# A four-layer graph network on one core: edge units in two fp16 parts, tanh moved in front of the scatter, a softmax without row maxima

## The chip, the core and the metric

The kernel runs on one core of a Trainium2 chip. The engines named below are TensorE (PE for its matmuls, PEld for its weight loads), VectorE (DVE), ScalarE (ACT), GpSimd (POOL) and SyncE (SP, which issues the DMAs here). Each engine works through its own queue in order, and the engines wait for each other with semaphores. The metric is the device time in microseconds of one execution; the value for a kernel is the median of its runs.

## What is computed

The input is x, 16 batches of 1024 nodes with 128 features, and adj, 16 weighted adjacency matrices of 1024 x 1024, of which some 1.5% are not zero. Four graph layers follow each other, each fed with the positive part of a layer norm of x and added to x. The change touches the third and the fourth:

```python
# layer 2, for l in range(2):
a = einsum('bnd,de->bne', x, We1[l, :D])
b = einsum('bnd,de->bne', x, We1[l, D:])
h = relu(a[:, :, None, :] + b[:, None, :, :] + be1[l])
scores = sigmoid(squeeze(h @ We2[l], -1) + be2[l])
messages = einsum('bnm,bmd->bnd', adjacency * scores, x)
...
# layer 3
e = (Wh1 + swapaxes(Wh2, 1, 2)) * (A + eye(N))
e = where(e >= 0, e, 0.2 * e)
scores = where(A + eye(N) > 0, e, -1e12)
h_prime = matmul(softmax(scores, axis=2), Wh)
```

The scores of layer 2 matter only where adj is not zero, so the kernel computes them for the edges alone.

## The kernel before

The adjacency matrix of a batch is cut into 128 x 128 tiles. A tile and its mirror image share their pattern, so there are 28 pairs off the diagonal and 8 diagonal tiles, 36 "buckets" in 9 groups of four (`GROUPS`: two diagonal groups, seven others). Each bucket has a fixed number of slots for its edges, 320 off the diagonal and 480 on it. For each batch `first` computes layers 0 and 1, counts the edges, and builds for each bucket one-hot matrices in fp8: `on`, `om` (node by slot) and their transposes `onT`, `omT`.

For each layer l of layer 2, `round` runs over the nine groups. `split` computes the two node terms a and b with We1 in float32 and cuts them into two fp16 parts (a rounded one and the rest, L715 and L716). `Group.gather` adds, for one bucket and one direction (two directions off the diagonal), the terms of the two ends of each edge with four fp16-by-fp8 matmuls into a PSUM bank `pre` (L810, L814; two banks in turn), and ScalarE takes the relu with the bias be1 into a float32 tile `hid` (L826). Each batch and layer has 64 such tiles. `Group.dots` takes four of them at a time, one set, and multiplies each with We2: the stationary operand is a 128 x 32 window of `slide`, in which only one column is not zero, so each product lands on one row of a strip of 32 rows of the bank `sc` (L838). The four strips are four column groups of the array. `Group.ends` copies the finished scores with be2 into `srow` (L856). In the next group's time `scores` turns them by matmul (L867), cuts each into two fp16 halves that lie in one 32-bit word, `u` (L872, L873), and spreads them over the one-hot matrix, `val` (L890, on VectorE): a multiplication of 0 or 1 by the word. `scatter` puts the scores in their places of a dense 128 x 512 tile with fp16 matmuls (L914), ScalarE takes tanh of it (L922), VectorE adds 1 and multiplies with the adjacency (L923), and `messages` multiplies with x in float32 (L930). A factor of 0.5 on the way out (L953) makes tanh a sigmoid.

`update` is the rest of a layer of layer 2. `last` does the second update and layer 3 (`layer3`), whose attention goes by 8 strips of 128 x 1024: L360 to L367 on VectorE, Exp on ScalarE with a sum along the row (L368), eight transposes (L372), eight matmuls (L243).

`run` weaves three lanes of program text for each batch b: `main(b)`, `last(b - 1)` and `first(b + 1)`. Each yields the cost of the piece it has just written, and `weave` takes the lane that has used the smallest share of its total (MAIN_US, LAST_US, FIRST_US). From this text each engine's order is laid out ahead of the run; the trace shows pieces of one lane, such as a set of dots, cut by pieces of another. Each lane has its own PSUM bank or banks ("pre" with two for m, "a" and "c" with one each).

At the end a flag says whether a bucket had more edges than slots; if so, a second path (`Pairs`) computes everything densely.

Of the kernel before, what the change touches and what calls it, by code (L numbers as in the profile page):

```python
# [22 lines left out]
C_OFF = 320  # L23
C_DIAG = 480

S_SCALE = 256.0
S_MAX = 60000.0

# [11 lines left out]

MAIN_US = 248.0
FIRST_US = 112.0
# [7 lines left out]
def tile_four_gnn_layers(  # L50
# [81 lines left out]
    nc.vector.tensor_copy(a2_bc, a3_sb[:, 1:2].to_broadcast([P, P]))  # L132

    slide = const.tile([P, L, 2 * G - 1], F32, name="slide")
    nc.vector.memset(slide, 0.0)
    for l in range(L):
        nc.vector.tensor_copy(slide[:, l, G - 1 : G], we2_sb[:, l : l + 1])

# [30 lines left out]
    class Layers:  # L169
# [121 lines left out]
        def update(self, l, xf, xfT, msgT, dst, name):  # L291
# [40 lines left out]
            yield 3  # L332

        def layer3(self, xt, row, name):

# [19 lines left out]
            for t in range(T):  # L355
                at = row(t)
                own = at[:, t * P : (t + 1) * P]
                nc.vector.tensor_add(own, own, ident)
                e = flat(self.scratch(f"e_{name}_{t}"))
                nc.vector.scalar_tensor_tensor(  # L360
                    e, wh2, wh1[:, t : t + 1], at, op0=OP.add, op1=OP.mult
                )
                nc.vector.tensor_scalar(at, at, 0.0, L3_NEG, op0=OP.is_le, op1=OP.mult)
                nc.vector.scalar_tensor_tensor(e, e, L3_ALPHA, e, op0=OP.mult, op1=OP.max)
                nc.vector.tensor_add(e, e, at)
                nmax = self.small([P, 1], "nmax", f"nmax_{name}_{t}")
                nc.vector.tensor_reduce(nmax, e, axis=AX.X, op=OP.max, negate=True)  # L367
                nc.scalar.activation(e, e, AF.Exp, bias=nmax, accum_out=rsum[:, 0, t : t + 1])  # L368
                attT = self.scratch(f"attT_{name}_{t}")
                for ks, ps in self.halves(f"attT_ps_{name}_{t}"):  # L370
                    for i, k in enumerate(ks):
                        nc.tensor.transpose(ps[:, i], e[:, k * P : (k + 1) * P], ident)  # L372
                    nc.scalar.activation(attT[:, ks[0] : ks[-1] + 1], ps, AF.Copy)
                hp = self.neighbours(attT, wh, f"3_{name}_{t}")
                nc.vector.reciprocal(rsum[:, 1, t : t + 1], rsum[:, 0, t : t + 1])
                nc.vector.tensor_scalar(o[:, t], hp, rsum[:, 1, t : t + 1], None, op0=OP.mult)
                yield 5
            neg = self.scratch(f"neg_{name}")
            nc.vector.tensor_scalar(neg, o, 0.0, None, op0=OP.min)
# [22 lines left out]
    class Batch:  # L402
        pass

    class Edges:
        def __init__(self, stack):
            self.work = stack.enter_context(tc.tile_pool(name="work", bufs=2))
            self.con = stack.enter_context(tc.tile_pool(name="con", bufs=1))
            self.hot = stack.enter_context(tc.tile_pool(name="hot", bufs=1))
            self.dram = stack.enter_context(  # L410
                tc.tile_pool(name="dram", bufs=2, space=bass.MemoryType.DRAM)
            )
            self.psum = stack.enter_context(
                tc.tile_pool(name="psum", bufs=1, space=bass.MemoryType.PSUM)
            )

            own = {"m": ("pre", 2), "a": ("a", 1), "c": ("c", 1)}
            self.m, self.a, self.c = (
                Layers(self.work, v, N_SCRATCH[v], self.psum, [own[v]]) for v in LANES
            )  # L420
            self.alone = [own[v] for v in ("a", "m", "c", "m")]
            self.constants()
# [14 lines left out]
        def constants(self):  # L437
# [32 lines left out]
            self.scale_terms()  # L470
            self.slide = con.tile([P, L, 2 * G - 1], F32, name="slide_s")
            for l in range(L):
                nc.vector.tensor_scalar(
                    self.slide[:, l], slide[:, l], unit[:, 1, l : l + 1], S_SCALE,
                    op0=OP.mult, op1=OP.mult,
                )
            self.be2 = con.tile([P, L], F32, name="be2_s")
            nc.vector.tensor_scalar(self.be2, be2_bc, S_SCALE, None, op0=OP.mult)

# [6 lines left out]
        def scale_terms(self):  # L486
# [18 lines left out]
            for l in range(L):  # L505
# [6 lines left out]
            nc.vector.tensor_reduce(  # L512
                bnd, ps[:, : 2 * L].rearrange("p (l h) -> p l h", h=2), axis=AX.X, op=OP.max
            )
            ps = self.a.one("bound_t")
            nc.tensor.transpose(ps[:L, :P], bnd, ident)
# [19 lines left out]
            nc.vector.tensor_copy(unit.rearrange("p i l -> p (i l)"), ps[:, : 2 * L])  # L536
            scale_layer(0)

        def load(self, lane, src, name):
# [170 lines left out]

        def split(self, xfT, w, name):

            parts = self.work.tile([P, 2, T, 2, D], F16, tag="part", name=f"part_{name}", bufs=1)
            for sl, ps in self.m.both(xfT, w, name):
                nc.scalar.activation(parts[:, 0, sl], ps, AF.Copy)  # L715
# [3 lines left out]
        def round(self, s, l, xf, xfT, name):  # L719


            pa, pb = self.split(xfT, we1_sb[:, l], name)
            msg = self.acc(f"msg_{name}")
# [36 lines left out]
        class Group:  # L760
# [41 lines left out]
            def gather(self, i, pa, pb):  # L802
# [4 lines left out]
                for d, (ra, rb) in enumerate((((pa, t), (pb, u)), ((pb, t), (pa, u)))[: self.nd]):  # L807
# [9 lines left out]
                    if not self.diag:  # L817
                        hid = path.work.tile(
                            [P, C_OFF], F32, tag="hid", name=f"hid_{self.name}_{i}_{d}", bufs=N_HID
                        )  # L820
                    elif i % 2 == 0:
                        self.two = flat(path.m.scratch(f"hid_{self.name}_{i}"))
                        hid = self.two[:, :HALF]
                    else:
                        hid = self.two[:, HALF:]
                    nc.scalar.activation(  # L826
                        hid[:, :c], pre[:, :c], AF.Relu, bias=be1_sb[:, self.l : self.l + 1]
                    )
                    self.hid.append(hid)

            def dots(self):
# [3 lines left out]
                while len(self.hid) - self.done >= J:  # L835
                    r = self.done // J
                    for g in range(J):
                        nc.tensor.matmul(  # L838
                            self.sc[g * G : (g + 1) * G, : self.c],
                            self.path.slide[:, self.l, G - 1 - r : 2 * G - 1 - r],  # L840
                            self.hid[self.done + g][:, : self.c],
                            start=(r == 0), stop=(r == self.per - 1),
                        )
                    self.done += J

            def ends(self):
# [8 lines left out]
                for dst, src in parts:  # L855
                    nc.vector.tensor_scalar(  # L856
                        dst, src, self.path.be2[:, self.l : self.l + 1], S_MAX, op0=OP.add, op1=OP.min
                    )

            def scores(self):  # L860
# [5 lines left out]
                for k in range(ck):  # L866
# [4 lines left out]
                u2 = u.bitcast(F16).rearrange("p (c r h) -> p c r h", r=per, h=2)  # L871
                nc.vector.tensor_scalar(u2[:, :, :, 1], pt, -S_MAX, None, op0=OP.max)  # L872
                nc.vector.scalar_tensor_tensor(  # L873
                    u2[:, :, :, 0], pt, -S_MAX, u2[:, :, :, 1], op0=OP.max, op1=OP.subtract
                )
# [6 lines left out]
                for d in range(self.nd):  # L882
                    for i in range(Q):
                        if i % 2 == 0:
# [4 lines left out]
                        right = (self.s.omT if d else self.s.onT)[self.grp[i]]  # L889
                        nc.vector.tensor_tensor(  # L890
                            pair[:, i % 2, :ck], right[:, :ck],
                            u[:, :, j % J, j // J : j // J + 1].to_broadcast([P, ck, P]), op=OP.mult,
                        )
                        self.val[d, i] = pair[:, i % 2]

            def scatter(self, part):

                each = self.rows // Q  # L900
                for j in range(part * each, (part + 1) * each):
# [16 lines left out]
                    if i == Q - 1:  # L918
                        upd = self.path.work.tile(
                            [P, Q, P], F32, tag="upd", name=f"upd_{self.name}_{d}"  # L920
                        )
                        nc.scalar.activation(upd, self.ps[d], AF.Tanh, scale=0.5 / S_SCALE)  # L922
                        nc.vector.scalar_tensor_tensor(  # L923
                            upd, upd, 1.0, self.adj[:, d * Q : (d + 1) * Q], op0=OP.add, op1=OP.mult
                        )
# [18 lines left out]
        def main(self, s, b):  # L944
# [3 lines left out]
            for l in range(L):  # L948
# [3 lines left out]
                s.msgT = lane.scratch(f"msgT_{name}")  # L952
                nc.vector.tensor_scalar(flat(s.msgT), self.msg, 0.5, None, op0=OP.mult)  # L953
                if l + 1 == L:
# [163 lines left out]
    with ExitStack() as stack:  # L1118
        path = Edges(stack)
        path.run()  # L1120

        over = path.work.tile([P, 2], F32, name="over")
        nc.vector.tensor_scalar(over[:, 0:1], path.most[:, 0:1], 2.0 * C_OFF, None, op0=OP.is_gt)
        nc.vector.tensor_scalar(over[:, 1:2], path.most[:, 1:2], 2.0 * C_DIAG, None, op0=OP.is_gt)
        ps = path.m.one("over_ps")
        nc.tensor.matmul(ps[:1, :2], ident[:, P - 1 : P], over, start=True, stop=True)
        nc.vector.tensor_reduce(flag, ps[:1, :2], axis=AX.X, op=OP.max)

# [41 lines left out]
```

## Time and profile before

| | us |
|---|---|
| median of 3 runs (5927.56 to 5934.77) | 5927.58 |
| profiled execution, its own time | 5932.83 |
| its span, first to last instruction | 5931.1 |
| hid, relu on ScalarE (L826), 2048 times | 1104.1 busy |
| pre, gather on TensorE (L810 and L814), 8192 times | 978.3 and 966.7 busy |
| dots (L838), 512 sets of 8 instructions | 676.1 busy |
| val on VectorE (L890), 2048 times | 606.6 and 440.1 busy |
| tanh behind the scatter on ScalarE (L922), 512 times | 305.7 busy |

The granted clock of TensorE was 0.980 over the span. Busy time counts an instruction from its start to its end; neighbours overlap, and a group's busy time is the time in which at least one of it runs. PE's busy time includes the time in which results leave the array, so it is an upper bound for the work itself. A float32 matmul appears as two instructions. In a line of a group the columns are: engine, operation, output and inputs by the program's names, sizes and types, count, then busy time, mean length in ns, and the engine's idle time just before the group's instructions, with what ended it.

### The profile page before, as it was taken

To read this page: it belongs to the slowest core of one execution; us is meant where nothing else is said; L and a number is where in the kernel's file an instruction comes from. 1 tells how busy PE (TensorE), PEld (TensorE's weight loads), DVE (VectorE), ACT (ScalarE), POOL (GpSimd) and SP (SyncE) were. 2 spreads that over 40 slices of the span, in tenths; PEclk is the share of its full clock that TensorE was granted. 3 is DMA by queue.
4 is the path that set the end of the run, shared out by engine and by line. 5 is a ranking of instruction groups with operands and counts; after the bars stand their busy time and mean duration, and the time that the engine had idled before them with its cause. 6 is when DMAs were issued, how large, how long until landed. Compare 5 with 4: busy or idle time off the path is not lost.

```text
span 5931.1 us, 112266 instructions
## 1 busy us (share of the span) xinstructions
PE 5518.9 (93%) x46080; PEld 3910.8 (66%) x46080; DVE 4248.2 (72%) x8138; ACT 3057.9 (52%) x5859; POOL 173.3 (3%) x105
## 2 busy tenths in 40 slices
PE   4899999999999999999999999999999999999985
PEld 4666667666676666667666676666667666676653
DVE  4566777867678686777867678686777867678665
ACT  2545464554646455474554646455374554646442
POOL 0000000000000000000000000000000000000000
PEclk8999999999999999999999999999999999999997
DMA  5322414233142422414233142432414233142110
GB/s 150 100 83 79 121 58 123 91 100 107 52 138 75 120 91 83 125 58 123 91 97 108 50 139 79 115 96 80 128 58 121 93 97 107 51 139 72 45 63 29
DMA packets 694154, 554.34 MB, mean 93 GB/s; under 512 B 29440, under 2 KB 630144, under 8 KB 693632
## 3 DMA queue, kind: packets, MB, share of 16 engines
q1 hardware_dynamic: 688384, 545.37, 30.8%
q8 instruction: 364, 5.96, 0.4%
q10 hardware_dynamic: 5248, 1.71, 0.2%
q14 instruction: 158, 1.29, 0.1%
HBM read 446.31 MB, written 100.66 MB: 92 GB/s over the span
## 4 chain that ended last, share of the span: by engine, by line
PE 65%; DVE 21%; ACT 5%; DMA 4%; issue 3%; POOL 2%; ACTq 0%; SPq 0%; DVEq 0%; POOLq 0%
PE sc L838 9%; PE p L914 7%; PE pre L810 7%; PE pre L814 7%; PE nb L243 6%; PE msg L930 5%; PE h L301 4%; DVE val L890 3%; PE bb L251 3%; PE pq L692 2%; PE pn L660 2%; PE xn L314 2%; POOL st L207 2%; PE pm L660 2%; PE tn L586 2%
## 5 line engine op out<-in xcount | busy, mean ns | idle before, releaser
L826 ACT ACTIVATE hid<-pre,be_sb 128x320 f32<-128x320 f32 (+1 forms) x2048 | 1104.1, 545 | 925.9 <-PE pre L814 913.1
L810 PE MATMUL pre<-on,part 128*128 128x320 fp8e4 (+1 forms) x4096 | 978.3, 308 | 20.0 <-ACT hid L826 10.5
L814 PE MATMUL pre<-om,part 128*128 128x320 fp8e4 (+1 forms) x4096 | 966.7, 307 | 0.0
L838 PE MATMUL sc<-hid,slide_s 128*32 128x320 f32 (+1 forms) x4096 | 676.1, 461 | 1.6 <-DVE u L873 1.5
L930 PE MATMUL msg<-upd,xf 128*128 128x128 f32 (+3 forms) x2944 | 608.3, 327 | 4.1 <-DVE upd L923 3.8
L890 DVE TENSOR_TENSOR val<-onT,u 128x384 f32<-128x384 fp8e4 (+1 forms) x1152 | 606.6, 580 | 4.3
L810 PEld LDWEIGHTS <-part 128*128 128x128 f16 x4096 | 363.6, 98 | 301.1 <-issue 233.8
L914 PE MATMUL p<-val,omT 128*128 128x128 f16 x6528 | 547.7, 218 | 2.0 <-DVE val L890 0.2
L814 PEld LDWEIGHTS <-part 128*128 128x128 f16 x4096 | 394.9, 98 | 173.5 <-issue 25.0
L914 PEld LDWEIGHTS <-omT 128*128 128x128 fp8e4 x6528 | 441.9, 96 | 68.9 <-issue 19.7
L696 DVE TENSOR_TENSOR omT<-pq,odd_off 128x384 fp8e4<-128x384 f32 x448 | 248.1, 554 | 318.4 <-PE pq L692 312.7
L890 DVE TENSOR_TENSOR val<-omT,u 128x384 f32<-128x384 fp8e4 x896 | 440.1, 549 | 0.0
L923 DVE SCALAR_TENSOR_TENSOR upd<-upd,adj 128x512 f32<-128x512 f32 x512 | 351.5, 686 | 112.3 <-ACT upd L922 108.5
L930 PEld LDWEIGHTS msg<-upd,xf 128*128 128x128 f32 x2944 | 399.4, 191 | 27.0 <-DVE upd L923 8.8
L922 ACT ACTIVATE upd<-p 128x512 f32<-128x512 f32 x512 | 305.7, 597 | 189.8 <-PE p L914 176.9
L856 DVE TENSOR_SCALAR srow<-sc,be_s 128x128 f32<-128x128 f32 (+2 forms) x512 | 217.1, 449 | 242.0 <-PE sc L838 240.0
L703 ACT ACTIVATE om<-pm 128x320 fp8e4<-128x320 f32 (+1 forms) x576 | 266.9, 464 | 212.3 <-PE pm L660 207.5
L689 ACT ACTIVATE onT<-pn 128x384 fp8e4<-128x384 f32 (+1 forms) x576 | 295.1, 513 | 128.0 <-PE pn L660 126.8
L914 PE MATMUL p<-val,onT 128*128 128x128 f16 x4480 | 354.4, 218 | 4.7 <-ACT upd L922 4.6
L914 PEld LDWEIGHTS <-onT 128*128 128x128 fp8e4 x4480 | 294.9, 96 | 49.2 <-issue 20.5
L360 DVE SCALAR_TENSOR_TENSOR e<-wh,wh,a 128x1024 f32<-128x1024 f32 x128 | 163.7, 1279 | 197.9 <-PE attT_ps L372 180.4
L243 PEld LDWEIGHTS nb<-z,ct 128*128 128x128 f32 x2048 | 251.1, 197 | 66.1 <-issue 45.6
(195 smaller groups left out, 9188.4 us busy)
## 6 DMA issues: line engine op xcount, KB each, us to landing
at<-in_adj_dram SPq DMA_DIRECT2D x128, 512.0 KB, 3.9
ct<-in_adj_dram SPq DMA_DIRECT2D x128, 512.0 KB, 4.1
a<-in_adj_dram SPq DMA_DIRECT2D x128, 512.0 KB, 3.4
adjT<-tn SPq DMA_DIRECT2D x128, 512.0 KB, 4.8
l<-adjT SPq DMA_DIRECT2D x128, 512.0 KB, 4.3
adj<-adjT SPq DMA_DIRECT2D x256, 256.0 KB, 3.5
adj<-adjT SPq DMA_DIRECT2D x384, 64.0 KB, 2.9
adj<-adjT SPq DMA_DIRECT2D x128, 192.0 KB, 3.0
```

Of the source, the lines that this page charges most:

```text
L243: nc.tensor.matmul(ps, mat[:, k], z[:, k], start=(k == 0), stop=(k == T - 1))
L689: nc.scalar.activation(onT, pn[:, : ck * P], AF.Copy, saturate=False)
L703: nc.scalar.activation(om, pm[:, :c], AF.Copy, saturate=False)
L810: nc.tensor.matmul(pre[:, :c], ra[0][:, k, ra[1]], on[:, :c], start=(k == 0), stop=False)
L814: nc.tensor.matmul(pre[:, :c], rb[0][:, k, rb[1]], om, start=False, stop=(k == 1))
L826: nc.scalar.activation(hid[:, :c], pre[:, :c], AF.Relu, bias=be1_sb[:, self.l : self.l + 1])
L838: nc.tensor.matmul(self.sc[g * G : (g + 1) * G, : self.c], self.path.slide[:, self.l, G - 1 - r : 2 * G - 1 - r], self.hid[self.done + g][ ...
L890: nc.vector.tensor_tensor(pair[:, i % 2, :ck], right[:, :ck], u[:, :, j % J, j // J : j // J + 1].to_broadcast([P, ck, P]), op=OP.mult,)
L914: nc.tensor.matmul(self.ps[d][:, i], left[:, k], halves[:, k, :, h], start=(k, h) == terms[0], stop=(k, h) == terms[-1],)
L922: nc.scalar.activation(upd, self.ps[d], AF.Tanh, scale=0.5 / S_SCALE)
L923: nc.vector.scalar_tensor_tensor(upd, upd, 1.0, self.adj[:, d * Q : (d + 1) * Q], op0=OP.add, op1=OP.mult)
L930: nc.tensor.matmul(self.msg[:, lo * P : hi * P], self.xf[:, mb], up, start=False, stop=True, skip_group_check=True,)
```

## The change

In words:

- **We2 folded into We1.** Since relu(v) w = sign(w) relu(v |w|), the columns of We1 and be1 are multiplied by |We2| at the start, and `slide` holds only the signs -1, 0 and 1.
- **Edge units in two fp16 parts.** be1 is now added in `split`, on the node term b, by an addition in PSUM. `gather` takes the relu without a bias on ScalarE into an fp16 tile, and the rest (the relu of pre less that part) on VectorE into a second fp16 tile. `dots` multiplies both parts with the signs in fp16.
- **tanh in front of the scatter.** `ends` is a tanh on ScalarE with bias and scale; `scores` cuts tanh times 256 in two halves; behind the scatter ScalarE has nothing to do, and VectorE reads the scatter's bank.
- **val on two engines.** Every second bucket's `val` is made on ScalarE, one activation of 128 columns for each 128 slots.
- **Layer 3 without row maxima** (class `Lane`): no subtraction of the maximum, and the mask is multiplied in behind Exp, with the sum of the row. A further condition of the flag (`fine`) says whether every row sum and its reciprocal are at most 1e30.
- **The weave's weight** MAIN_US is 215 in place of 248. Some constants change with these.

```diff
-MAIN_US = 248.0
+MAIN_US = 215.0
...
+    with tc.tile_pool(name="fold", bufs=1) as fold:
+        mag = fold.tile([P, L, D], F32, name="we2_mag")
+        nc.scalar.dma_start(mag, we2.rearrange("l d o -> (o l) d")[None].broadcast_to([P, L, D]))
+        nc.scalar.activation(mag, mag, AF.Abs)
...
+        for l in range(L):
+            nc.vector.tensor_mul(
+                we1_sb[:, l], we1_sb[:, l], mag[:, l, None, :].to_broadcast([P, 2, D])
+            )
...
+    class Lane(Layers):
...
+        def weights(self, e, at, total, name):
+            nc.vector.scalar_tensor_tensor(e, e, L3_ALPHA, e, op0=OP.mult, op1=OP.max)
+            nc.scalar.activation(e, e, AF.Exp)
+            nc.vector.scalar_tensor_tensor(
+                e, at, 0.0, e, op0=OP.is_gt, op1=OP.mult, accum_out=total
+            )
...
-                nc.vector.tensor_scalar(at, at, 0.0, L3_NEG, op0=OP.is_le, op1=OP.mult)
-                nc.vector.scalar_tensor_tensor(e, e, L3_ALPHA, e, op0=OP.mult, op1=OP.max)
-                nc.vector.tensor_add(e, e, at)
-                nmax = self.small([P, 1], "nmax", f"nmax_{name}_{t}")
-                nc.vector.tensor_reduce(nmax, e, axis=AX.X, op=OP.max, negate=True)
-                nc.scalar.activation(e, e, AF.Exp, bias=nmax, accum_out=rsum[:, 0, t : t + 1])
+                self.weights(e, at, rsum[:, 0, t : t + 1], f"{name}_{t}")
...
-            for sl, ps in self.m.both(xfT, w, name):
+            for sl, ps in self.m.both(xfT, we1_sb[:, l], name):
+                nc.vector.tensor_add(ps[:, :, 1], ps[:, :, 1], over_t(self.be1[:, l], 2))
...
-                            [P, C_OFF], F32, tag="hid", name=f"hid_{self.name}_{i}_{d}", bufs=N_HID
+                            [P, 2, C_OFF], F16, tag="hid", name=f"hid_{self.name}_{i}_{d}", bufs=N_HID
...
-                    nc.scalar.activation(
-                        hid[:, :c], pre[:, :c], AF.Relu, bias=be1_sb[:, self.l : self.l + 1]
+                    nc.scalar.activation(hid[:, 0, :c], pre[:, :c], AF.Relu)
+                    nc.vector.scalar_tensor_tensor(
+                        hid[:, 1, :c], pre[:, :c], 0.0, hid[:, 0, :c], op0=OP.max, op1=OP.subtract
                     )
...
-                    for g in range(J):
-                        nc.tensor.matmul(
-                            self.sc[g * G : (g + 1) * G, : self.c],
-                            self.path.slide[:, self.l, G - 1 - r : 2 * G - 1 - r],
-                            self.hid[self.done + g][:, : self.c],
-                            start=(r == 0), stop=(r == self.per - 1),
-                        )
+                    for v in range(2):
+                        for g in range(J):
+                            nc.tensor.matmul(
+                                self.sc[g * G : (g + 1) * G, : self.c],
+                                self.path.slide[:, self.l, G - 1 - r : 2 * G - 1 - r],
+                                self.hid[self.done + g][:, v, : self.c],
+                                start=(r == 0 and v == 0), stop=(r == self.per - 1 and v == 1),
+                            )
...
-                    nc.vector.tensor_scalar(
-                        dst, src, self.path.be2[:, self.l : self.l + 1], S_MAX, op0=OP.add, op1=OP.min
+                    nc.scalar.activation(
+                        dst, src, AF.Tanh, bias=self.path.be2[:, self.l : self.l + 1],
+                        scale=self.path.down[:, self.l : self.l + 1],
                     )
...
-                        nc.vector.tensor_tensor(
-                            pair[:, i % 2, :ck], right[:, :ck],
-                            u[:, :, j % J, j // J : j // J + 1].to_broadcast([P, ck, P]), op=OP.mult,
-                        )
+                        v = u[:, :, j % J, j // J : j // J + 1]
+                        if i % 2:
+                            for k in range(ck):
+                                nc.scalar.activation(
+                                    pair[:, 1, k], right[:, k], AF.Copy, scale=v[:, k]
+                                )
+                        else:
+                            nc.vector.tensor_tensor(
+                                pair[:, 0, :ck], right[:, :ck], v.to_broadcast([P, ck, P]), op=OP.mult
+                            )
...
-                        nc.scalar.activation(upd, self.ps[d], AF.Tanh, scale=0.5 / S_SCALE)
                         nc.vector.scalar_tensor_tensor(
-                            upd, upd, 1.0, self.adj[:, d * Q : (d + 1) * Q], op0=OP.add, op1=OP.mult
+                            upd, self.ps[d], S_SCALE, self.adj[:, d * Q : (d + 1) * Q],
+                            op0=OP.add, op1=OP.mult,
                         )
```

## The prediction

> **What bounds the kernel now.** I read four views, from coarse to fine. First the page: busy time by engine, and the chain of work that ended last.
>
> ```profile
> PE 5518.9 (93%) x46080; PEld 3910.8 (66%) x46080; DVE 4248.2 (72%) x8138; ACT 3057.9 (52%) x5859; POOL 173.3 (3%) x105
> ...
> PE 65%; DVE 21%; ACT 5%; DMA 4%; issue 3%; POOL 2%; ACTq 0%; SPq 0%; DVEq 0%; POOLq 0%
> ```
>
> TensorE is the bound, VectorE second: of 5931 us the chain runs 65% through PE, 21% (1246 us, 29% of DVE's busy time) through DVE, 5% (297 us, 9.7% of ACT's) through ACT. Second, the same chain in order of time, in the middle of a batch (start, length, work):
>
> ```profile
> 2232.95 0.66 PE sc L838 x2
> 2233.61 0.27 PE pn L660 x3
> 2233.88 0.67 PE sc L838 x6
> ...
> 2237.45 0.50 PE msg L930 x4
> ...
> 2238.25 0.27 PE pre L810 x2
> ...
> 2240.45 0.68 PE sc L838 x8
> ```
>
> Work follows work without gaps. An fp16-by-fp8 pass of 320 columns (pre) takes 0.135. A float32 matmul is two instructions of two passes each: msg's 128-column instruction takes 0.125, where fp16 passes of the scatter take 0.057 (ten in 0.57, elsewhere in this view). Most telling is sc: two, six or eight of its instructions take the same 0.66 to 0.68, so the four strips of 32 columns run side by side, and a burst costs four passes (0.54) plus 0.13. One set (four strips, eight instructions) is often cut in two bursts with other work between. Third, the groups by shape (busy, mean ns, idle before):
>
> ```profile
> L826 ACT ACTIVATE hid<-pre,be_sb 128x320 f32<-128x320 f32 x1792 | 935.7, 529 | 864.6 <-PE pre L814 855.1 <-PE pq L692 2.3 <-PE po L622 0.3
> L838 PE MATMUL sc<-hid,slide_s 128*32 128x320 f32 x3584 | 551.1, 445 | 1.6 <-DVE u L873 1.5
> L890 DVE TENSOR_TENSOR val<-onT,u 128x384 f32<-128x384 fp8e4 x896 | 443.8, 551 | 3.7
> L647 ACT ACTIVATE far<-iota_off,mid 128x384 f16<-128x384 f16 x448 | 267.4, 617 | 4.0 <-DVE on L651 4.0
> L365 DVE TENSOR_TENSOR e<-e,a 128x1024 f32<-128x1024 f32 x128 | 155.5, 1215 | 0.1
> L716 DVE TENSOR_TENSOR part<-bb,part 128x512 f16<-128x512 f32 x128 | 87.1, 687 | 29.2 <-ACT part L715 28.1
> L262 ACT ACTIVATE z<-bb 128x256 f32<-128x256 f32 x64 | 24.5, 383 | 56.5 <-PE bb L251 56.5
> ```
>
> ACT waits for PE before hid: it has room. Fourth, the stretches of one batch (a batch is about 356 us), PE, PEld, DVE, ACT busy of 12:
>
> ```profile
> 2314.00:2326.00 12.00, 11.79 (x83) 6.20 (x80) 5.15 (x10) 5.99 (x12) 0.00 (x0) 1.00 0.01 1
> ...
> 2362.00:2374.00 12.00, 12.00 (x112) 8.78 (x110) 11.46 (x22) 5.69 (x11) 0.00 (x0) 1.00 0.58 168
> ```
>
> In 9 of 30 such stretches DVE is over 11.2 of 12 busy: it has no room there, and much in the others.
>
> **The dots (PE).** 512 sets: 448 of 320 columns (3584/8), 64 of 480. Now busy 551.1 + 125.0 = 676 us; on the chain 8.9% = 528. Afterwards a strip takes two fp16 passes instead of four. In one burst a set costs 2 x 0.135 + 0.13 = 0.40 (480 columns: 0.54), 214 us in all; in two bursts, one per part, 0.53 and 0.67, 280; if each part is cut again, 1.06 and 1.34, 561. Saved: against busy time 462, 396 or 115; against the chain's 528, 314, 248 or a loss of 33. The high part is ready an instruction earlier than the low one, so I expect two bursts, between 396 and 248, nearer the first, since a burst off the chain holds PE too: **-360**.
>
> **The second part (DVE), new:** 2048 scalar_tensor_tensor from PSUM. The nearest row is L716, same types, 687 at 512 columns; L890's forms (551 at 384, 683 at 512) give 1.03 ns a column, so 489 at 320 and 654 at 480: 876 + 167 = 1043. In a run, four val take 1.95, which is 64 ns less each: 912. I take 980.
>
> **What DVE loses:** every second val goes to ACT, half of 1046.7, -523. ends() goes to ACT: -229.7 (107.6 + 76.5 + 45.6). Layer 3 drops L363, L365 and L367 (88.0 + 155.5 + 154.9) and gains one masked multiply with a sum, priced as L364's 1217 ns x 128 = 156, at most 180 with a read of the sum like ACT's 189 ns: -235. split() gains 128 adds of be1, 422 ns each by L263: +54. upd (686 ns) keeps its shape and now reads PSUM; u, msgT likewise: nothing. Sum **+46**, from -22 to +117.
>
> **ACT.** hid loses its bias column; a bias costs 90 ns (L305's 687 against L373's 597 at 512): -184. The odd val become 28 x 3 + 4 x 4 = 100 activations of 128 columns per layer and batch, 3200. No row has this shape. From below L262, PSUM without a column, less 128 columns at 0.86 ns: 276 ns, 883 us. From above L647, SBUF and a column, less 256 at 0.81: 409, 1309 us. It is nearer L647; some overlap between neighbours: 360, 1150 us. tanh in front of the scatter: -305.7 (L922); on the score rows 224 of 256 columns, 224 of 128 and 64 of 480, with two columns each 90: 563, 456, 748 ns, +276. Exp without bias and accumulator: 128 x (90 + 189) = -36. Sum **+900**, from +633 to +1059: ACT to about 3960 us, 70%.
>
> The Trainium skill (ScalarE: Activation LUTs, Rules for kernel authors) advises VectorE, not ScalarE, for a plain multiply, which speaks against this move. In this case's rows it is dear too: about 1.1 us of ACT for 0.55 of DVE. That page's figures (186 ns, 93 a column, 0.833 per element) would make it an estimated 386 ns, 1235 us, or +985 in all and 8 us more in the sum; no run shows the shape yet.
>
> **On the path.** At the shares that the chain has of these engines, ACT's +900 costs 0.097 x 900 = +87 and DVE's +46 costs 0.29 x 46 = +13. The cover is PE's own queue of other lanes; without it, +900 on ACT would come whole. hid now passes ACT (0.44) and then DVE (0.49) before the second half of the dots; behind the waiting matmul stand the next gathers, and behind them everything on PE. Today PE waits for hid only some 18 us (10.5 and 6.6 in its two queues).
>
> **Ends of the run.** The last batch's layer 3 (from 5837 us) is uncovered: the chain takes 9.7 us a strip. Off it come L365 and L367, on it comes 1.22, and Exp gives up 0.28: -1.5, with L363 -2.2; eight strips, **-14**. The prologue gains a 128 KB load and a dozen small operations, 0 to 8: **+4** (a small weight's load takes 5.0 now). MAIN_US moves only the order: main's yields sum to 248.6, so with 215 the other lanes are written out by 86% of main. It may fill the 24 us at a batch's start where PE is busy 16.8 (at most -115), or leave main's end alone, where PE would idle as in 5780 to 5850 us (38.7 of 70): 0.14 x 330 us a batch x 0.45 x 16 = +330. I take 0, between ends that I can't weigh.
>
> **Sum:** 5931 - 360 + 87 + 13 - 14 + 4 = 5661. The profiled execution took 5932.8 around its span, the median of the runs is 5927.6, some 5 less: **5655**.
>
> **Rivals.** (a) ACT and DVE stay hidden whole and sets go in one burst: 5931 - 462 - 14 - 5 = 5450. For it: PE's idle groups name hid hardly at all. Against: DVE's 21% of the chain. (b) DVE decides in its full stretches, 30% of the batch: there 38 of 128 low parts (0.48 each) cost 18 us, the val moved give back 10: +8 x 16 = +128 on the forecast, 5785. For it: the second row above; against: layer 3's 15 us a batch come off just there. (c) **Slower:** pre has two banks, each held today by four matmuls and one relu, then also by the DVE subtraction, which queues behind 1.2-us operations. If PE stops at L810 for the bank once per pair of gathers, 1024 times, by 0.49 and half a 1.22-us operation, that is 1126 us; against 360 - 90 saved it decides from 0.26 a pair on. At half the price: 5931 + 563 - 270 = 6220. For it: DVE's full stretches; against: PE has some 4.6 us of work per pair. (d) It doesn't do what it says: sets cut in four bursts save between 115 and -33, and ACT's price stays: about 5980.
>
> **Chances.** Forecast 0.47 (5560 to 5750), (a) 0.18, (b) 0.17, (c) 0.13, (d) 0.05. About 0.2% (12 us) is what a measurement can tell from no change. Faster: forecast, (a) and nearly all of (b), 0.81; within 0.2%: 0.03 from the edges of (b) and (d); slower 0.16. The range reaches from just under (a) to the end of (b), 5430 to 5900, and leaves out (c) and most of (d).
>
> **What would show it.** Dots: L838's successor busy near 280 us. The low parts near 480 ns, DVE's total near 4290 us, ACT's near 3960, its val groups near 360 ns. (c) shows as PE waiting at pre for DVE's hid. I am wrong if the bursts are cut finer, if PE's waits on DVE grow past some 200 us, or if the new flag for large sums were set, which would run the whole other path; the inputs' scale gives no ground for that.

## The result, and the profile after

| | before | after |
|---|---|---|
| median of 4 runs, us | 5930.95 | 6276.55 |
| lowest and highest, us | 5927.56, 5934.77 | 6264.19, 6280.16 |
| span of the profiled execution, us | 5931.1 | 6276.9 |

The ratio is 1.0579, with a 95% interval from 1.056 to 1.0597: 346 us slower, where 5655 us was forecast. The page of the changed kernel, busy time and chain:

```profile
PE 5638.0 (90%) x46082; PEld 4031.5 (64%) x46082; DVE 4361.2 (69%) x8726; ACT 3692.6 (59%) x8934; POOL 197.6 (3%) x105
...
PE 64%; DVE 19%; ACT 8%; DMA 4%; issue 3%; POOL 2%; SPq 0%; ACTq 0%; DVEq 0%; POOLq 0%
```

TensorE, which was to lose 360 us, is busy 119 us longer. The groups by shape (busy, mean ns, idle before) say that the single prices were not the trouble:

```profile
L887 DVE SCALAR_TENSOR_TENSOR hid<-pre,hid 128x320 f16<-128x320 f32 x1792 | 842.9, 485 | 388.0 <-ACT hid L886 378.3
...
L956 ACT ACTIVATE val<-onT,u 128x128 f32<-128x128 fp8e4 x1856 | 591.1, 393 | 92.4 <-DVE u L936 90.8 <-DVE u L942 0.3
L900 PE MATMUL sc<-hid,slide 128*32 128x320 f16 x3584 | 542.9, 310 | 14.0 <-ACT hid L886 9.9 <-DVE hid L887 2.5
```

The low part takes 485 ns where 489 was worked out. A val on ScalarE lasts 393 ns; without the overlap of neighbours it is 319 (1020.8 us for 3200), where 360 was taken. But the dots are busy 542.9 us, and 551.1 before, with half the passes. The chain in order of time shows why (start, length, work):

```profile
2404.48 0.17 PE p L982 x3
2404.65 0.25 PE sc L900 x4
2404.90 0.84 PE msg L998 x2
2405.74 0.17 PE pn L716 x3
2405.91 0.24 PE sc L900
2406.15 0.38 PE pre L868 x2
...
2407.51 0.24 PE sc L900 x2
2407.76 0.27 PE pm L716 x3
2408.03 0.28 PE msg L998 x2
2408.30 0.24 PE sc L900
```

One matmul of a 32-column strip takes 0.24 or 0.25 of the chain, and so do four; the pair of pre behind it takes 0.38 where a pair elsewhere takes 0.27. So a run of dots, however short, costs some 0.2 us beside its passes, and the sets are cut into far more runs than before. The prediction's 0.13 a burst is only the half that lies within the run. The other half stood one line below the last one that it showed of the kernel before, behind the set at 2240.45, where this pair takes 0.38 in place of 0.27:

```profile
2241.12 0.38 PE pre L810 x2
```

Counted in the order of PE's queue (an uninterrupted row of dots is one run; a set before is 4 matmuls, after 8):

```
before: 2048 matmuls in  836 runs: 309 of one, 43 of two, 283 of three, 201 of four
after:  4096 matmuls in 1871 runs: 1031 of one, 234 of two, 189 of three, ... 18 of eight
```

That is 1.6 runs a set before and 3.7 after, where I had expected two. The second thing stands between main's two rounds, where its first update and that update's layer norm lie (the prediction called this place a batch's start, which it is not). Stretches of 12 us (PE, PEld, DVE, ACT busy):

```profile
2267.00:2279.00 12.00, 3.47 (x19) 2.35 (x17) 10.47 (x14) 2.29 (x4) 2.96 (x2) 0.73 0.15 48
2279.00:2291.00 12.00, 8.52 (x40) 6.92 (x40) 9.59 (x15) 3.66 (x7) 2.12 (x1) 0.70 0.31 117
```

PE is busy 12 of 24 us there, against 16.8 before, and VectorE 20 of 24, against 23 before. The same place in the kernel before:

```profile
2134.00:2146.00 12.00, 8.17 (x69) 7.55 (x68) 11.37 (x16) 2.44 (x4) 1.64 (x1) 1.00 0.56 178
2146.00:2158.00 12.00, 8.65 (x28) 5.90 (x29) 11.58 (x15) 4.14 (x7) 0.00 (x0) 0.72 0.41 144
```

Over the whole span PE's idle time (span less busy) grows from 412 to 639 us. The granted clock of the span is 0.958, and 0.980 before. A pair of pre takes 0.27 in both chains, so the gathers keep their pace; what the lower clock costs elsewhere, no run separates.

### The profile page after: what moved, and what is told of

It is laid out like the page before. It is cut to its first block, busy times and chain, and to the rows that moved or that the text cites. A ratio compares the mean times of both kernels' runs of the same rounds, so it can differ in the third digit from the quotient of the medians.

```text
span 6276.9 us, 116119 instructions
## 1 busy us (share of the span) xinstructions
PE 5638.0 (90%) x46082; PEld 4031.5 (64%) x46082; DVE 4361.2 (69%) x8726; ACT 3692.6 (59%) x8934; POOL 197.6 (3%) x105
## 4 chain that ended last, share of the span: by engine, by line
PE 64%; DVE 19%; ACT 8%; DMA 4%; issue 3%; POOL 2%; SPq 0%; ACTq 0%; DVEq 0%; POOLq 0%
PE nb L259 9%; PE pre L868 8%; PE p L982 7%; PE pre L872 7%; PE sc L900 6%; PE msg L998 6%; PE h L317 4%; DVE val L960 3%; PE bb L267 2%; DVE hid L887 2%; ACT val L956 2%; PE xn L330 2%; PE pn L716 2%; PE attT_ps L395 2%; PE tn L642 2%
## 5 line engine op out<-in xcount | busy, mean ns | idle before, releaser
L887 DVE SCALAR_TENSOR_TENSOR hid<-pre,hid 128x320 f16<-128x320 f32 (+1 forms) x2048 | 1007.7, 506 | 492.0 <-ACT hid L886 481.8
L886 ACT ACTIVATE hid<-pre 128x320 f16<-128x320 f32 (+1 forms) x2048 | 891.1, 450 | 566.9 <-PE pre L872 500.0
L868 PE MATMUL pre<-on,part 128*128 128x320 fp8e4 (+1 forms) x4096 | 976.6, 311 | 48.9 <-DVE hid L887 42.6
L900 PE MATMUL sc<-hid,slide 128*32 128x320 f16 (+1 forms) x4096 | 634.4, 318 | 28.4 <-ACT hid L886 20.5
L956 ACT ACTIVATE val<-onT,u 128x128 f32<-128x128 fp8e4 x1856 | 591.1, 393 | 92.4 <-DVE u L936 90.8
L956 ACT ACTIVATE val<-omT,u 128x128 f32<-128x128 fp8e4 x1344 | 429.7, 391 | 0.0
L990 DVE SCALAR_TENSOR_TENSOR upd<-p,adj 128x512 f32<-128x512 f32 x512 | 349.9, 683 | 86.0 <-PE p L982 77.7
L900 PEld LDWEIGHTS <-slide 128*32 128x32 f16 x4096 | 188.6, 93 | 329.5 <-issue 196.5
L918 ACT ACTIVATE srow<-sc,be_s,down 128x128 f32<-128x128 f32 (+2 forms) x512 | 252.8, 538 | 234.5 <-PE sc L900 232.3
L707 DVE TENSOR_SCALAR on<-far,wid 128x384 fp8e4<-128x384 f16 (+1 forms) x576 | 248.0, 432 | 195.5 <-PE pre L868 176.6
L259 PE MATMUL nb<-wh,attT 128*128 128x128 f32 x2048 | 316.7, 308 | 25.6 <-ACT attT L396 25.6
```

Of the source, the lines that this page charges most:

```text
L259: nc.tensor.matmul(ps, mat[:, k], z[:, k], start=(k == 0), stop=(k == T - 1))
L868: nc.tensor.matmul(pre[:, :c], ra[0][:, k, ra[1]], on[:, :c], start=(k == 0), stop=False)
L886: nc.scalar.activation(hid[:, 0, :c], pre[:, :c], AF.Relu)
L887: nc.vector.scalar_tensor_tensor(hid[:, 1, :c], pre[:, :c], 0.0, hid[:, 0, :c], op0=OP.max, op1=OP.subtract)
L900: nc.tensor.matmul(self.sc[g * G : (g + 1) * G, : self.c], self.path.slide[:, self.l, G - 1 - r : 2 * G - 1 - r], self.hid[self.done + g][ ...
L918: nc.scalar.activation(dst, src, AF.Tanh, bias=self.path.be2[:, self.l : self.l + 1], scale=self.path.down[:, self.l : self.l + 1],)
```

## The experiments

T1: the cut sets. T2: the weave's weight. T3: the work that came to VectorE and ScalarE (the low part, val, tanh, the addition of be1). Every time is compared with runs of the kernel before on the same chip (5928 to 5932 us).

**Whole sets, on the changed kernel.** The last strip's low part is written first, and the matmuls of a set keep their order in the queue, so that none should stand before all inputs are there.

```diff
-                    for v in range(2):
-                        for g in range(J):
+                    for v in (1, 0):
+                        for g in reversed(range(J)):
...
-                                start=(r == 0 and v == 0), stop=(r == self.per - 1 and v == 1),
+                                start=(r == 0 and v == 1), stop=(r == self.per - 1 and v == 0),
```

> The changed kernel, but the eight matmuls of a set of dots are written in reverse: the low part of the last strip first, so none can be placed before all eight inputs are there. Nothing is left out. In the order of PE's queue the 512 sets then stand in 609 uninterrupted runs, where the changed kernel has 1871 and the kernel before 836. Theory T1 (cut sets: each run of dots pays some 0.11 us to leave the column groups, and runs of one matmul use one strip of four): the dots' busy time falls from 634 to about 250 us, and the time by 150 to 390 us, to 5890 to 6130. Rival T2 (the weave's weight leaves main's end without cover) and rival T3 (the relu, its low part and val are late on ScalarE and VectorE): the dots' busy time falls too, but the time stays above 6200, because PE then waits elsewhere.

Measured: 6137.66 us, ratio 1.035 (1.0332 to 1.0367), 139 us less. Its groups, with both shapes of the dots in one line:

```profile
L900 PE MATMUL sc<-hid,slide 128*32 128x320 f16 (+1 forms) x4096 | 272.1, 316 | 19.9 <-DVE hid L887 17.0
```

The 512 sets now stand in 609 runs, nearly whole. The dots' busy time falls by 362 us, from 634.4 to 272.1, as T1 has it. The time falls by 139, a little short of T1's 150, because much of the rest turns into waits: PE's idle time grows from 639 to 797 us, and of the chain PE holds 52%, DVE 25% and ACT 13%, where it was 64, 19 and 8.

**Whole sets, on the kernel before.**

```diff
-                    for g in range(J):
+                    for g in reversed(range(J)):
```

> The kernel before with the four strips of a set of dots written in reverse, so that a set is one run (526 runs in place of 836). Nothing is left out. T1 (a run costs 0.67 us whatever its number of strips): the dots' busy time falls from 676 to about 390 us, and the time by 100 to 250 us, to 5680 to 5830. If the sets that were cut cost nothing on the path, within 1% of 5931.

Measured: 5737.58 us, ratio 0.9676 (0.966 to 0.9692). The chain in order of time of this run shows whole sets, the groups the sum:

```profile
2312.31 0.73 PE sc L838 x8
...
2319.10 0.74 PE sc L838 x8
```

```profile
L838 PE MATMUL sc<-hid,slide_s 128*32 128x320 f32 (+1 forms) x4096 | 409.0, 461 | 7.0 <-DVE u L873 2.1 <-ACT hid L826 0.3
```

A line's change takes 267 us off the dots and 193 off the time. The kernel before had the same flaw, with fewer runs, and lost more time by it than the changed kernel does (193 against 139). So the cut sets explain why the forecast gain did not come, but not why the changed kernel is slower than the kernel before: with whole sets in both it is 6138 against 5738, 400 us slower.

**The weave's weight, both ways.**

```diff
# the changed kernel
-MAIN_US = 215.0
+MAIN_US = 248.0
# the kernel before
-MAIN_US = 248.0
+MAIN_US = 215.0
```

> The changed kernel with MAIN_US back at 248. Nothing is left out. T2 (weave's weight): the stretch at a batch's start, in which PE is busy 20 of 36 us now and 17 of 24 before, shrinks, and the time falls by 8 to 15 us a batch, to 6040 to 6150. T1 (cut sets): the runs of dots go from 1871 to 1748, so 20 to 40 us less, about 6245. T3: within 0.5% of 6277.

> The kernel before with MAIN_US at 215 alone. Nothing is left out. T2: slower than 5931 by 100 to 250 us, 6030 to 6180. T1 and T3: within 1% of 5931 (the runs of dots go from 836 to 788, some 20 us less).

Measured: 6096.5 us (1.0277, 1.026 to 1.0294) for the first, 180 less; 6129.38 us (1.0336, 1.0319 to 1.0353) for the second, 198 more. T2 holds in both directions, as far as the time goes. The second kernel's stretches between main's rounds, then its chain there, and what its TensorE waited for (us, times, longest):

```profile
2209.00:2221.00 12.00, 3.90 (x19) 2.94 (x18) 9.19 (x12) 1.19 (x2) 2.54 (x1) 0.64 0.11 34
2221.00:2233.00 12.00, 5.03 (x22) 4.08 (x21) 11.26 (x15) 3.31 (x6) 1.64 (x1) 0.50 0.31 113
```

```profile
2210.89 1.12 DVE st L205
2212.01 1.13 DVE y L202
...
2215.94 1.23 DVE xf L222
2217.17 1.13 DVE sq_y L204
2218.30 0.60 DVE a L363
2218.91 1.13 DVE st_y L205
2220.04 1.13 DVE e L364
...
2227.62 1.13 DVE xf L330
```

```profile
PE tp L214 <- DVE xf L222: 117.5, 16, 12.6
PE tp_xf L214 <- DVE xf L330: 106.4, 15, 10.7
```

In the kernel before, the same two waits are:

```profile
PE tp_xf L214 <- DVE xf L330: 61.8, 16, 6.0
...
PE tp L214 <- DVE xf L222: 17.5, 16, 12.6
```

xf of L222 ends the norm with which `first` goes into layer 2, xf of L330 the norm of main's first update. With 215 they take turns on VectorE, with a strip of layer 3 between them (a L363, e L364), and PE, which has neither gathers nor builds until one of them is done, stands still. The cause can be read in the text: main's update lies between 112 and 137 of main's 248.6, the norm of `first` between 64 and 70 of its 112. At 248 that is 0.45 to 0.55 against 0.57 to 0.63, one behind the other; at 215 it is 0.52 to 0.64, both at once. PE's idle time grows by 189 us (412 to 602), nearly the whole 198, and these two waits by 145.

In the changed kernel the chain also shows the two norms in turns at this place, but the two waits do not account for its 180 us: that for the norm of `first` is 117.5 with 215 and 29.3 with 248, that for main's update 5.1 and 94.4, together 122.6 and 123.7. There PE is idle for 75 us less with 248, spread over many waits, and busy for 109 less, of which 39 are dots. So the weight's cost is shown for both kernels, and its cause for the kernel before alone.

**Both together, then val back, then the low part away.** The third kernel keeps one float32 hid, as before the change, and multiplies it in float32 with the signs. The second's edit on top of the first, and the core of the third's:

```diff
# second
-                        if i % 2:
+                        if False:
...
-                                pair[:, 0, :ck], right[:, :ck], v.to_broadcast([P, ck, P]), op=OP.mult
+                                pair[:, i % 2, :ck], right[:, :ck], v.to_broadcast([P, ck, P]), op=OP.mult
# third
-                    nc.scalar.activation(hid[:, 0, :c], pre[:, :c], AF.Relu)
-                    nc.vector.scalar_tensor_tensor(
-                        hid[:, 1, :c], pre[:, :c], 0.0, hid[:, 0, :c], op0=OP.max, op1=OP.subtract
-                    )
+                    nc.scalar.activation(hid[:, :c], pre[:, :c], AF.Relu)
```

> The changed kernel with both edits so far: MAIN_US back at 248 and the dots in reverse, one run a set. Nothing is left out. T1 and T2 add up: 6277 - 139 - 180 = 5958, 5920 to 5990. Rival T3a (with the sets whole, PE waits for the low part and for val, on VectorE and ScalarE): less of it comes through, 6000 to 6090.

> The same with every val on VectorE again, as before the change: ScalarE loses about 1020 us of busy time, VectorE gains some 520. Nothing is left out. T3b (ScalarE's small activations hold up the relu and srow behind them): 60 to 150 us less than the run with both edits. T3c (VectorE is what holds PE up): 50 to 150 us more.

> The changed kernel with MAIN_US 248, with hid in one float32 part as before (one relu on ScalarE, no low part on VectorE) and the dots in float32 against the signs, one run a set. Nothing else is undone, nothing is left out. VectorE loses about 1000 us of busy time, the dots' busy time on TensorE rises from some 250 to some 400. T3c (the low part on VectorE is dearer than what it saves on TensorE): 80 to 200 us less than the run with both edits. If TensorE is what counts: 80 to 150 us more.

Measured: 5950.06 us (1.0033, 1.0022 to 1.0044); 6085.51 us (1.0257, 1.024 to 1.0275); 5805.32 us (0.9782, 0.9765 to 0.98). T1 and T2 add up (5958 was the sum), against T3a. The rest of the change does not beat the kernel before, though, on equal terms: with whole sets that takes 5738. With the low part there, VectorE's time counts: val back on it costs 135 us, against T3b. Without the low part it takes 145 us less, against "TensorE is what counts", although the dots rise from 254.6 to 399.0. First the kernel with both edits, then the one without the low part:

```profile
PE 5235.4 (88%) x46082; PEld 3883.2 (65%) x46082; DVE 4301.6 (72%) x8726; ACT 3650.4 (61%) x8934; POOL 173.6 (3%) x105
...
PE 52%; DVE 21%; ACT 12%; DMA 8%; issue 4%; POOL 2%; ACTq 0%; SPq 0%; DVEq 0%; POOLq 0%
```

```profile
PE 5297.1 (91%) x46082; PEld 3867.6 (67%) x46082; DVE 3446.6 (59%) x6678; ACT 3630.8 (63%) x8934; POOL 175.1 (3%) x105
...
PE 56%; DVE 15%; ACT 14%; DMA 8%; issue 3%; POOL 2%; SPq 0%; ACTq 0%; DVEq 0%; POOLq 0%
```

VectorE loses 855 us and its share of the chain falls from 21% to 15%. PE is busy for only 62 us more, and idle for 202 less (704 to 502). With the low part, two of PE's waits are:

```profile
PE p L982 <- DVE upd L990: 55.1, 68, 1.4
PE pre L868 <- DVE hid L887: 53.7, 124, 1.9
```

Without it the first is 10.9 and the second is gone. So the low part costs both ways, by holding the banks of pre and by making other work on VectorE late, and it costs more than the cheaper dots save (144 us of the dots' busy time).

**Layer 3 alone, and a heavier weight.** On the kernel before with whole sets: class `Lane` and the flag's third condition as in the change; then MAIN_US at 265.

```diff
-                nc.vector.tensor_scalar(at, at, 0.0, L3_NEG, op0=OP.is_le, op1=OP.mult)
-                nc.vector.scalar_tensor_tensor(e, e, L3_ALPHA, e, op0=OP.mult, op1=OP.max)
-                nc.vector.tensor_add(e, e, at)
...
+                self.weights(e, at, rsum[:, 0, t : t + 1], f"{name}_{t}")
```

> The kernel before with the dots in one run a set (5738 us) and layer 3 as in the change (no row maxima, the mask behind Exp, the new condition of the flag). Nothing is left out. VectorE loses some 240 us of busy time in stretches where it is full: at the share of the chain (26%) 60 us less and 14 at the end, 5640 to 5690. If the gain lies off the path: 5715 to 5740.

> The kernel before with whole sets and the new layer 3 (5691 us) and MAIN_US at 265 in place of 248: the main lane is written out earlier than the others. Nothing is left out. If the time falls all the way with this weight (215 cost 198 us on the kernel before): 5600 to 5670. If 248, where main's shares add up to its total, is the best place: 5700 to 5800.

Measured: 5691.35 us (0.9595, 0.9579 to 0.9611), the fastest of all, 46 less than whole sets alone, where 74 were expected, and 1 us above the expected 5640 to 5690. With 265: 5720.11 us (0.9644, 0.9624 to 0.9664), 29 more, as was given for 248 as the best place of the two.

**What is left: val, tanh, be1.** All on the kernel with float32 dots and no low part (5805 us). Its edits: val on VectorE (as above); tanh behind the scatter; both.

```diff
+                    nc.vector.tensor_scalar(
+                        dst, src, self.path.down[:, self.l : self.l + 1],
+                        self.path.be2[:, self.l : self.l + 1], op0=OP.mult, op1=OP.add,
+                    )
...
+                        nc.scalar.activation(upd, self.ps[d], AF.Tanh, scale=1.0 / S_SCALE)
```

> The run with float32 dots and no low part (5805 us; MAIN_US 248, one run a set), and every val on VectorE again. Nothing is left out. 5805 is still 114 us over the kernel before with whole sets and the new layer 3 (5691), from which it differs by val on two engines, tanh in front, the fold with be1 in split, and the relu without bias. If the val on ScalarE (1.1 us in three pieces for 0.55 us) hold up relu and srow in its queue: 60 to 120 us less, 5685 to 5745. If VectorE is still what counts, as with the low part there: 50 us more or above.

> The same run with float32 dots, and tanh behind the scatter again, with ends on VectorE (val stay on both engines). Nothing is left out. If the new place of tanh costs (srow now waits in ScalarE's queue, behind val): 20 to 70 us less, 5735 to 5785. If it pays, since upd has one step less: 10 to 50 us more.

> Both undone on the run with float32 dots: what is left of the change is the fold of We2, be1 added in split, the relu without bias, and layer 3. Nothing is left out. If val and tanh are the whole rest: 5680 to 5710, the 5691 of the kernel before with whole sets and the new layer 3. If the addition in split or the fold costs: above 5720.

Measured: 5811.87 us (0.98, 0.9784 to 0.9817); 5847.61 us (0.9868, 0.9851 to 0.9884); 5807.91 us (0.9799, 0.9783 to 0.9816). The first met neither case: where VectorE has room, it is all one where val is made. The second says that tanh in front pays, 42 us beside val on ScalarE; the third, that it pays nothing measurable when val is back, and that the addition or the fold costs. Why the two places of tanh differ only beside val on ScalarE is not shown. So 117 us to 5691 were open, and the last two runs took be1 back out of split:

```diff
-                nc.vector.tensor_add(ps[:, :, 1], ps[:, :, 1], over_t(self.be1[:, l], 2))
...
-                    nc.scalar.activation(hid[:, :c], pre[:, :c], AF.Relu)
+                    nc.scalar.activation(
+                        hid[:, :c], pre[:, :c], AF.Relu, bias=be1_sb[:, self.l : self.l + 1]
+                    )
```

> The run with float32 dots, val on VectorE and tanh behind (5808 us), and be1 again as the relu's bias on ScalarE: the 128 additions in split are gone. Nothing is left out. Against the kernel before with whole sets and the new layer 3 (5691 us) only the fold of We2 at the start, a scale in ends and where some constants lie differ. If the addition in split costs (it stands between the matmul and the first fp16 part, four times a layer, where PE has little else): 5680 to 5720. If not, 5790 to 5820, and the rest lies in the order of the queues or the prologue.

> The run with float32 dots (5805 us, val on both engines, tanh in front) with be1 as the relu's bias and no addition in split. Nothing is left out. If the addition in split costs about 110 us: 5680 to 5720, and as tanh in front paid 42 us beside val on two engines, perhaps below 5691. If not: 5790 to 5850, above 5805 where the bias's 90 ns on 2048 relus (184 us of ScalarE) count.

Measured: 5723.91 us (0.9656, 0.964 to 0.9672), 84 less than with the addition; 5737.01 us (0.9678, 0.9662 to 0.9694), 68 less. The addition, 128 times 428 ns, 54.6 us in all, costs more than its length, although the relu with a bias is the longer one (544 ns against 453). In the chain of the kernel with the addition (val and tanh as before), between main's rounds:

```profile
2117.00 1.14 DVE e L436
2118.14 1.13 DVE st L216
2119.26 0.40 DVE deg L637
2119.66 0.65 issue
2120.31 0.21 DVE bb L772
...
2122.32 0.68 PE attT_ps L395 x4
2123.00 0.02 issue
2123.01 1.98 PE bb L267 x8
2124.99 0.02 issue
2125.02 0.43 DVE bb L772
2125.45 1.12 DVE sq L220
2126.57 1.20 DVE part L774 x2
```

The addition (bb L772) is a second visit to VectorE between the matmul and the first part, behind operations of 1.1 us. The same kernel's list of what the makers and readers of `part` waited for, as far as it goes by that addition:

```profile
  DVE bb L772: 97.0, 97
```

For 97 us ScalarE sat idle in front of a first part until the addition was done. Without the addition the first part follows the matmul, and in place of this entry the list has:

```profile
  PE bb L267: 46.7, 81
```

That the addition costs its 84 and 68 us by where it stands is argued from these rows. PE's waits for `part` itself are 8 us with it and 10 without; its idle time is 486 and 445, and the largest single difference is a wait of layer 3's transposes, 66.8 against 39.1. In the first run 29 fewer runs of dots (555 to 526) add 20 us of dots to the difference; in the second the sets are whole with and without. The expected 5680 to 5720 was missed by 4 us in the first run, and the second lies between its two cases.

## Why the prediction was wrong, step by step

The changed kernel and its steps back, each on top of the one above:

| step | us | difference |
|---|---|---|
| changed kernel | 6276.6 | |
| MAIN_US 248 | 6096.5 | -180 |
| whole sets | 5950.1 | -146 |
| no low part, float32 dots | 5805.3 | -145 |
| val and tanh as before | 5807.9 | +3 |
| be1 as a bias again | 5723.9 | -84 |

The end lies below the kernel before (5931), because whole sets and the new layer 3 stay in. On equal terms, with whole sets in both, the changed kernel is 400 us slower (6138 against 5738), and the steps, with the runs of the kernel before, tell where: 188 by the weight (6138 to 5950), 145 by the low part less what the cheaper dots save, 84 by be1 in split, 33 open, val and tanh -3, layer 3 -46.

**The dots, "two bursts, between 396 and 248", the term -360: failed.** The chain's row gave the price of a run (0.67 for four passes); the traces bore it out, with 0.1 us more on the instruction behind. What failed is the number of runs: 3.7 a set, near the four of rival (d), because eight inputs that come ready one by one, from two engines, were each given their place as they came. Instead of 360, the busy time fell by 42 (676.1 to 634.4). The chain that I showed had sets of two and six in it; the reason for the cut was there to be asked for. One of the signs of being wrong, bursts that are cut finer, is what came. Whole sets alone would not have saved the forecast, though: they take 139 us off 6277.

**MAIN_US, "I take 0": failed, and is the largest term of the loss.** 198 us on the kernel before, 180 on the changed one. The upper bound of 330 was on paper, with a cause at main's end; on the kernel before the loss came between main's rounds, in the very 24 us where I had looked for a gain of 115, having taken them for a batch's start. Between two ends so far apart, 0 was a choice without a row behind it.

**The low part, "+46" for VectorE's sum, +13 on the path: the size of the low part held, its price did not.** It took 1007.7 us against 980. VectorE grew by 113 in all, near the end of the range given (-22 to +117; its own terms give -30 to +126). But the work taken away and the work added do not have the same price. With the low part there, moving 455 us of val to VectorE (4301.6 to 4757.2) costs 135 us, 0.30 of it, just the chain's share of 0.29 that I had used. Without the low part 454 us (3446.6 to 3900.8) cost 7. The saving in layer 3 (191 us of VectorE, 4236.8 to 4046.0) was worth 46. A net sum hides that the low part stands between relu and dots for every edge unit, while val does not press when VectorE has room. With whole sets the second part took 144 us off the dots (399.0 to 254.6) and put 145 on the time.

**ACT, "+900, +87 on the path": too high, and harmless.** ScalarE grew by 635 us (3057.9 to 3692.6), with val at 1020.8 in place of 1150 and the relu 213 less where 184 was taken. (The lower bound for a val, 276 ns, is 273 by its own terms, which changes nothing.) Val on ScalarE costs nothing measurable where VectorE has room (5805 against 5812) and saves 135 where it has none. The Trainium skill (ScalarE: Activation LUTs, Rules for kernel authors) would have kept the multiply on VectorE; here the measurement decides against the rule when VectorE is the fuller engine. The same page's figures for one such activation (What ACT_TABLE_LOAD costs; an estimated 386 ns) agree with the 393 and 391 measured.

**split, "+54" of VectorE: size right, effect 84 us.** It was priced as busy time alone; the 55 us on VectorE were right, and 84 on the time is what taking it out gave.

**The rivals.** (c), 1126 us or half of it, happened only in small: PE's idle time at pre until the low part was there is 42.6 us in all, in 61 waits, and 93.6 with whole sets. (d)'s mechanism did happen, joined by the weave, which no rival carried; both slow rivals lay largely outside the range. (a) and (b) had the dots' saving as their ground and fell with it.

What stays open: 33 us between 5724 and 5691, between which lie the fold, a scale in ends and the prologue; by what path the weight costs the changed kernel 180 us; and how the low part's cost divides between VectorE's queue and the longer hold on pre's two banks. A third bank for pre would tell; it was not tried.

## What to carry to other kernels

Before a cheaper instruction is counted, count the runs it will stand in: matmuls of column strips paid some 0.2 us for each run here, and splitting their inputs by time splits the runs; writing the latest input first kept them whole and gave 193 us on the kernel before, the best single edit here. A parameter that only orders work is a term of the sum like any other; when its bounds lie 445 us apart, the forecast's range should have them. A flaw that both kernels have must be mended in both before the change is judged: whole sets gave the kernel before more than the changed one. And an engine's busy time has a price only together with its place: the same 455 us cost 135 or 7.

## What the hardware showed that was not expected

A single 128 x 32 matmul of 320 columns holds the chain for 0.24 us, as do two or four side by side, and the next full-width pair takes 0.38 in place of 0.27. Six to eight (up to four strips, two passes each) take 0.38 to 0.45 in the run with whole sets. The Trainium skill (TensorEngine Tiling (Array Packing), Key Properties) says that a change of tiling mode drains the engine, and names no time. Some 0.1 us on either side of a run, as here, would fit; no run separates the drain from other causes. At 1871 runs in place of 609 that makes an estimated 250 us of TensorE. The dots' busy time fell by 362, since a run of one strip takes as long as one of four, and 139 came through.
